# A layer of a graph network on Trainium2: three of six column chunks summed over fetched lists instead of by dense products

## The chip, the cores and the metric

The kernel runs on one core of a Trainium2 chip. A core has TensorE (PE, matmuls), VectorE (DVE), ScalarE (ACT), GpSimd (POOL) and SyncE (SP, which only issues DMAs here); each runs its instructions in order, and they meet through semaphores. The metric is the device time of one execution in microseconds. The kernel before took 2341.08 us, the median of three runs (2340.66 to 2345.28).

## The reference

There are N = 2708 nodes with D = 512 features. `adj` is a symmetric matrix of zeros and ones; about 0.6% of its entries are one. Four layers follow each other, each with a residual and a layer norm:

```python
x = _layernorm(x + _L0_gnn_ref(...))   # relu(((dinv (A+I) dinv) x + x) W + b)
x = _layernorm(x + _L1_gnn_ref(...))   # (dis A dis x) W.T + b
x = _layernorm(x + _L2_gnn_ref(...))   # two attention layers, softmax(scores) * adj
x = _layernorm(x + _L3_gnn_ref(...))   # A (x W) + b, heads side by side
```

Layer 3 can be computed as `(A x) W + b`: a sum of the neighbours' rows, then one product with a 512x512 matrix. That sum is what the change is about.

## The kernel before

The 2708 rows are cut into 22 blocks of 128 rows, the last with 20. The columns of A (the nodes that receive) are cut into six chunks of 512, 512, 512, 512, 384 and 276 (`CH`, L28). The blocks (the nodes that give) are taken in six groups of 4, 4, 4, 4, 3 and 3 (`GROUPS`, L30). A step is one chunk and one group, written (k, g) below.

*Dense sums.* Layers 0, 1 and 3 sum densely. `load` brings the bytes of A for a step, `prepare` turns them into weights `m` on ScalarE, and `multiply` (L849) accumulates, for each block and each of four slices of 128 features, two matmuls: one with the high and one with the low part of x (`xh`, `xl`). The result `acc` is the transposed sum. `evict` copies it to `ht`, `project` (L936) multiplies by W (`mm`), `combine` (L976) adds the residual `xres` and the bias, and `finish` does the layer norm and writes the rows. The bytes of A come from `masks`, written in layer 0.

*Lists.* The two attention layers do not sum densely. For each block of 128 receivers there are twelve lists of 128 givers: four with givers of the whole block and two for each quarter of 32 receivers; the last block has three lists. A list is fetched with one indirect DMA (`g<-pairs,givers`, a row per giver) on GpSimd, and multiplied with weights made from the row's softmax part. The indices of the givers (`givers`) are built during layer 1: `prepare` reduces the bytes of a group to one mark per giver and quarter (`feeds`, on VectorE), and after a chunk's last group `index` (L1097) ranks them, makes a one-hot table per block (`at_row`, `hit`, `both`, on VectorE) and multiplies it on TensorE (`list`). These jobs are spread over the following steps by `work`: one piece for VectorE or for TensorE after certain steps (`step`, L1043).

*Layer 1's surroundings.* In `step`, `before_products` first loads two steps ahead and prepares one step ahead, so VectorE's `feeds` reduce of step t+1 stands in its queue before what the step itself puts there: list tables, the ends of the chunk before (`combine`, LN), the evictions. On GpSimd's queue stand the writes of the finished rows (`x<-o`), of the transposed rows (`t<-x2t`, after ScalarE's copy) and the loads of the residuals (`xres<-x`). On TensorE's queue stand the dense products of the step, then a `list` product or transposes, then, at the chunk's end, the next chunk's.

*The tail.* While the second attention layer ends, `early` (L598) already runs the first twelve steps of layer 3: chunks 0 to 2 over groups 0 to 3; the half sums are copied away (`begun`). When the attention's last rows are there, `run` goes through the rest: groups 4 and 5 of chunks 0 to 2, then chunks 3 to 5 in full, all by `step`. Six chunk ends follow, each with four products with W per block and an LN of the chunk's blocks; the last chunk's three blocks are ended one by one after the last product.

*Order and memory.* Instructions are recorded through a wrapper (`Ordered`, L53), so that every instruction of this path has line L70 in the profile; they are told apart by the names of their tiles. Most tiles are pages of one ring of 82 (`PAGES`), fetched rows come into eleven wide tiles (`WIDES`), and the eight banks of the accumulator memory are split into two halves.

Of the kernel before, what the change touches and what calls it, by code (L numbers as in the profile page):

```python
# [41 lines left out]
PAGES, WIDES = 82, 11  # L42
TWO = 3
LN_EPS = 1e-5
DEG_EPS = 1e-8
SLOPE = 0.01


# [38 lines left out]
class Kernel:  # L87


    def __init__(self, ctx, tc, x_in, x_t, adj, adj_t, w0, b0, w1, b1, w2, w2_t, w3, b3, out):  # L90
# [26 lines left out]
        self.block = tile_("block", [P, NB], BF)  # L117
        self.since = tile_("since", [P, P], BF)
        self.saved = [
            [scratch.tile([P, D], FP, tag=f"x{s}_{i}", name=f"x{s}_{i}") for i in range(NB)]  # L120
            for s in range(3)
        ]
        self.between = [
            scratch.tile([P, D], FP, tag=f"y_{i}", name=f"y_{i}") for i in range(NB)
# [15 lines left out]
    def constants(self, page):  # L140
        nc = self.nc
        make_identity(nc, self.ident)
        nc.gpsimd.memset(self.ones, 1.0)
        nc.gpsimd.memset(self.ones_b, 1.0)
        nc.gpsimd.memset(self.feeds, 0.0)
        for q in range(QUARTERS):
            nc.gpsimd.memset(self.base[:, q : q + 1], float(q * ONLY * P - FAR))
        for dst, pattern, base, per_row in (
            (self.upto, [[1, P]], 0, 0),
            (self.node, [[0, 1]], 1 - P, 1),  # L150
            (self.block, [[1, NB]], 1 - NB, 0),
        ):
            w = dst.shape[1]
            whole = page("count", I32)[:, :w]
            nc.gpsimd.iota(whole, pattern=pattern, base=base, channel_multiplier=per_row)
            nc.gpsimd.tensor_copy(dst, whole)

        nc.gpsimd.memset(self.since, -1.0)
        nc.gpsimd.affine_select(
            out=self.since,  # L160
            in_=self.since,
            pattern=[[-1, P]],
            compare_op=ALU.is_ge,
            fill=0.0,
            base=0,
            channel_multiplier=1,
        )

    def load_w(self, pool, src, width, name, bufs=1):
# [344 lines left out]
class Fast:  # L514
# [17 lines left out]
    def run(self):  # L532
        kernel, nc = self.k, self.nc
        with ExitStack() as ctx:
# [23 lines left out]
            run.seq = [(l3, k, g) for k in range(TWO) for g in range(4)]  # L558
            run.seq += [(l3, k, g) for g in (4, 5) for k in range(2)]
            run.seq += [(l3, k, g) for k in range(2, TWO) for g in (4, 5)]  # L560
            run.seq += [(l3, k, g) for k in range(TWO, len(CH)) for g in range(len(GROUPS))]
            attention.run(self.early(run))
            for j in range(*GROUPS[5]):
                l3.rows[j] = attention.made[j]
            for t in range(4 * TWO, len(run.seq)):
                self.step(run, t)

            ly, k = run.before
            for i, n, ps in self.project(ly, k):
                self.finish(ly, k, [(i, n, self.combine(ly, i, n, ps))])  # L570

# [26 lines left out]
    def early(self, run):  # L598
# [7 lines left out]
        yield True  # L606
        for t in range(4 * TWO):
            ly, k, g = seq[t]
# [9 lines left out]
            self.prepare(*seq[t + 1])  # L618
            if g == 3:
                ly.begun[k] = []  # L620
            for n, j in enumerate(range(*GROUPS[g])):
                if t == 0:
                    self.multiply(ly, k, g, [j])
                else:
                    self.multiply(ly, k, g, ds=[n])
                self.attention.advance(2 * cost(CH[k][1]))
                if g == 3:
                    b = self.page(f"begun{k}_{n}")
                    self.nc.scalar.copy(b[:, : CH[k][1]], ly.acc[k][n][:, : CH[k][1]])
                    ly.begun[k].append(b)  # L630
                yield True


    def layernorm(self, rows):

# [9 lines left out]
        y = small.tile([P, DC], FP, tag="y", name="y")[:, :m]  # L645
        self.rsqrt(y, mv[:, :m, 1], LN_EPS)
        for q, (r, o, n) in enumerate(rows):
            nc.vector.tensor_scalar(
# [133 lines left out]
    def prepare(self, ly, k, g):  # L782
# [16 lines left out]
        if ly.number == 1:  # L799
            at, (j0, j1) = ly.done.pop(("bytes", k, g)), GROUPS[g]  # L800
            feeds = self.k.feeds.rearrange("p i q j -> p j (i q)")
            i0, full = c0 // QW, cw // QW
            sets = [(j0, j1, P)] if j1 < NB else [(j0, j1 - 1, P), (j1 - 1, j1, QW)]
            for q0, q1, n in ((0, full, QW), (full, -(-cw // QW), cw % QW)):
                for a, b, rows in sets if q0 < q1 else ():
# [5 lines left out]
                        ALU.max,  # L811
                    )

    def examine(self, ly, k, g, ats):
# [34 lines left out]
    def multiply(self, ly, k, g, only=None, ds=range(DC)):  # L849
        nc, cw = self.nc, CH[k][1]  # L850
        blocks = only or range(*GROUPS[g])
        two = ly.number == 3 and k < TWO
        starts, stops = ((0, 16), (15, NB - 2)) if two else ((0,), (NB - 2,))
        if blocks[0] in starts and 0 in ds:

            half = 0 if two and blocks[0] == 0 else k
            ly.acc[k] = [self.bank(half, f"acc{ly.number}_{k}_{d}") for d in range(DC)]
        ms = ly.done["m", k, g]
        if blocks[-1] == NB - 1:


            blocks = blocks[:-1]
            for x in (ly.hi, ly.lo):
                for d in range(DC):
# [4 lines left out]
                        ms[-1][few, :cw],  # L869
                        start=False,  # L870
                        stop=False,
                    )
        todo = [(d, j) for d in ds for j in blocks]
        if k == 0 and g + 1 < len(GROUPS):
# [61 lines left out]
    def project(self, ly, k):  # L936

        nc = self.nc
        parts = []
        for i, lo, n in blocks_of(k):  # L940
            if n <= QW:
                ps = self.few(
                    k,
                    f"mm{ly.number}_{i}",
                    n,
                    D,
                    lambda c: ly.ht[k][c][:, lo : lo + n],
                    lambda c: ly.w[c],
                )
                parts.append((i, n, ps))  # L950
                continue
            ps = self.bank(k, f"mm{ly.number}_{i}")
            for c in range(DC):
                nc.tensor.matmul(
                    ps[:n],
                    ly.ht[k][c][:, lo : lo + n],
                    ly.w[c],
                    start=(c == 0),
                    stop=(c == DC - 1),
                )  # L960
            parts.append((i, n, ps))
        return parts

    def residual(self, ly, k):
        for i, _, _ in blocks_of(k):
            t = self.page(f"xres{ly.number}_{i}")
            self.nc.gpsimd.dma_start(t, ly.source[i])
            ly.done["xres", i] = t

# [6 lines left out]
    def combine(self, ly, i, n, ps):  # L976

        nc, x = self.nc, ly.done.pop(("xres", i))
        if n <= QW:
            t = self.page(f"mm_sb{ly.number}_{i}")  # L980
# [13 lines left out]

    def finish(self, ly, k, parts):

        nc, out = self.nc, []
        for i, n, x in parts:
# [3 lines left out]
            out.append((i, o, n))  # L1002
        self.layernorm([(x, o, n) for (_, n, x), (_, o, _) in zip(parts, out)])
        for i, o, n in out:
# [270 lines left out]
class Attention:  # L1275
# [28 lines left out]
    def blank(self):  # L1304

        blank = [self.page(f"blank{e}") for e in range(2)]
        for e, t in enumerate(blank):
            self.nc.gpsimd.memset(t, 0.0)
            for pairs in (p for ly in self.pairs for p in ly):
                for r in range(2):  # L1310
                    c = e * D
                    w = min(D, D + 2 * P - c)
                    self.nc.sync.dma_start(pairs[r, N:, c : c + w], t[: NP - N, :w])

    def begin(self, step):
# [463 lines left out]


@with_exitstack
def kernel(
# [61 lines left out]
```

## Time and profile before

| what | us |
| --- | --- |
| median of three runs | 2341.08 |
| the profiled execution | 2338.2 |
| its span, first to last instruction | 2336.5 |
| TensorE busy | 2274.8 |
| VectorE busy | 1474.8 |
| GpSimd busy | 762.3 |
| ScalarE busy | 662.2 |
| mean granted TensorE clock | 0.993 |

The busy share of an engine is no measure of what bounds a stage; the chain of waits is: it follows the last instruction back, at each step to what released it. A row of the groups gives the line, the engine, the operation, the names of what is written and read with their shapes, the count, then busy time and mean, and after the second bar the idle time of the engine just before these instructions with its releaser. The largest group of GpSimd is the fetching of the attention layers:

```profile
L70 POOL DMA_INDIRECT g<-pairs,givers x510 | 516.2, 1012 | 897.0 <-DMA pairs<-s 537.4
```

Fetches come in a fixed rhythm where nothing holds them, here at the end of the second attention layer in GpSimd's timeline (start, length, what, and in brackets the idle time before):

```profile
2095.87 0.95 POOL L70 DMA_INDIRECT g<-pairs,givers  x1 [0.30 <-PE acc L70]
2097.12 0.94 POOL L70 DMA_INDIRECT g<-pairs,givers  x1 [0.30 <-PE acc L70]
2098.37 0.95 POOL L70 DMA_INDIRECT g<-pairs,givers  x1 [0.30 <-issue]
```

### The profile page before, as it was taken

How to read it: one execution, taken by the hardware profiler on the slowest of the kernel's cores; microseconds unless marked ns; L12 is line 12 of the kernel's file. 1: busy time of each engine (PE TensorE's matmuls, PEld its weight loads, DVE VectorE, ACT ScalarE, POOL GpSimd, SP SyncE). 2: the span in 40 equal slices, each digit the busy share in tenths (PEclk: the TensorE clock that was granted, in tenths of full speed). 3: DMA queues.
4: the chain of work that ended last, by engine and by line, in shares of the span. 5: the costliest groups of instructions: out<-in, count | busy, mean ns of one | idle time of the engine just before them, and what ended most of it. 6: DMA issues, size and time to landing. Idle time of an engine off the chain costs nothing.

```text
span 2336.5 us, 26171 instructions
## 1 busy us (share of the span) xinstructions
PE 2274.8 (97%) x8518; PEld 1292.5 (55%) x8518; DVE 1474.8 (63%) x2831; ACT 662.2 (28%) x1334; POOL 762.3 (33%) x879
## 2 busy tenths in 40 slices
PE   8999999999999999999999999999999999999997
PEld 6677677778644444443456444444443456566585
DVE  6999986786655529657677511228677788724523
ACT  6544353223100113222223200113232334432211
POOL 6645641111000000636375550000636466551000
PEclk9999999999999999999999999999999999999998
DMA  9765652222434404869699996405869799983311
GB/s 343 258 199 169 182 172 86 74 86 70 171 146 167 154 0 143 278 229 311 204 324 350 302 388 232 152 0 163 279 217 314 233 316 329 305 279 96 123 48 43
DMA packets 312440, 463.50 MB, mean 198 GB/s; under 512 B 60162, under 2 KB 189706, under 8 KB 312292
## 3 DMA queue, kind: packets, MB, share of 16 engines
q1 hardware_dynamic: 252276, 240.81, 31.5%
q0 software_dynamic: 60016, 220.92, 27.1%
q8 instruction: 69, 1.13, 0.2%
q14 instruction: 79, 0.65, 0.1%
HBM read 307.75 MB, written 153.85 MB: 198 GB/s over the span
## 4 chain that ended last, share of the span: by engine, by line
PE 84%; DVE 7%; DMA 4%; issue 2%; ACT 1%; POOL 1%; SPq 0%; DVEq 0%; ACTq 0%; POOLq 0%
PE sp L70 32%; PE acc L70 29%; PE mm L70 9%; PE z L70 6%; PE wst L70 6%; DMA pairs<-s 1%; DMA at<-in_adj_t 1%; DVE st L70 1%; DMA at<-mask 1%; ACT m L70 1%; DVE s L70 1%; PE list L70 1%; PE mix L70 0%; POOL bytes L70 0%; PE tr_x2t L70 0%
## 5 line engine op out<-in xcount | busy, mean ns | idle before, releaser
L70 POOL DMA_INDIRECT g<-pairs,givers x510 | 516.2, 1012 | 897.0 <-DMA pairs<-s 537.4
L70 PE MATMUL sp<-xs,wst_sb 128*128 128x512 f32 (+3 forms) x2112 | 797.7, 544 | 0.0
L70 PEld LDWEIGHTS sp<-xs,wst_sb 128*128 128x128 f32 (+1 forms) x2112 | 380.0, 186 | 406.8 <-issue 321.9
L70 PE MATMUL acc<-m,xh 128*128 128x512 f32 (+4 forms) x1584 | 571.4, 382 | 13.6 <-ACT m L70 7.0
L70 PE MATMUL acc<-m,xl 128*128 128x512 f32 (+4 forms) x1584 | 553.2, 367 | 1.5 <-DVE xl L70 1.5
L70 PEld LDWEIGHTS acc<-m,xh 128*128 128x128 f32 (+1 forms) x1584 | 290.3, 189 | 81.4 <-issue 22.3
L70 PEld LDWEIGHTS acc<-m,xl 128*128 128x128 f32 (+1 forms) x1584 | 290.3, 189 | 48.1 <-issue 5.7
L70 ACT COPY s<-sp 128x512 f32<-128x512 f32 (+2 forms) x252 | 133.6, 531 | 482.1 <-PE sp L70 469.5
L70 PE MATMUL acc<-g 128*32 128x512 f32 (+1 forms) x1020 | 260.8, 605 | 0.9 <-DMA g<-pairs,givers 0.5
L70 DVE TENSOR_TENSOR top<-top,s 128x512 f32<-128x512 f32 (+5 forms) x240 | 149.6, 623 | 170.6 <-ACT s L70 169.1
L70 PE MATMUL mm<-w,ht 128*128 128x512 f32 (+1 forms) x528 | 222.6, 593 | 8.1 <-DVE ht L70 8.1
L70 ACT CAST m<-at 128x512 fp32r<-128x512 uint8 (+5 forms) x396 | 199.2, 567 | 80.0 <-DMA at<-mask 63.7
L70 ACT ACTIVATE s<-s 128x512 f32<-128x512 f32 (+3 forms) x264 | 150.7, 580 | 236.6 <-DVE s L70 236.3
L70 DVE TENSOR_TENSOR sum<-sum,s 128x512 f32<-128x512 f32 (+4 forms) x252 | 157.4, 625 | 23.9 <-ACT s L70 23.9
L70 DVE TENSOR_TENSOR s<-s,a 128x512 f32<-128x512 f32 (+3 forms) x264 | 165.9, 628 | 10.2 <-DMA a<-mask 1.2
L70 DVE TENSOR_TENSOR s<-s,shift 128x512 f32<-128x512 f32 (+3 forms) x264 | 162.8, 620 | 6.7 <-ACT shift L70 6.7
L70 PEld LDWEIGHTS mm<-w,ht 128*128 128x128 f32 (+1 forms) x528 | 95.5, 186 | 124.4 <-issue 110.9
L70 PE MATMUL wst<-xt,mixed 128*128 128x512 f32 (+2 forms) x384 | 152.5, 550 | 1.7 <-ACT mixed L70 1.7
L70 PEld LDWEIGHTS acc<-g 128*32 128x32 f32 (+1 forms) x1020 | 75.4, 134 | 136.9 <-issue 115.8
L70 PE MATMUL z<-w,xt 128*128 128x512 f32 (+1 forms) x352 | 151.0, 596 | 0.0
L70 DVE COPY z_sb<-z 128x512 f32<-128x512 f32 (+1 forms) x44 | 30.3, 690 | 179.5 <-PE z L70 176.3
L70 POOL DMA_DIRECT2D x<-o x44 | 26.0, 596 | 358.0 <-DVE o L70 354.2
(167 smaller groups left out, 1657.4 us busy)
## 6 DMA issues: line engine op xcount, KB each, us to landing
pairs<-s SPq DMA_DIRECT2D x378, 128.0 KB
pairs<-z_sb SPq DMA_DIRECT2D x84, 512.0 KB
at<-in_adj_t SPq DMA_DIRECT2D x84, 256.0 KB
xres<-x POOLq DMA_DIRECT2D x44, 256.0 KB, 4.3
x<-o POOLq DMA_DIRECT2D x43, 256.0 KB, 3.1
x<-x SPq DMA_DIRECT2D x37, 256.0 KB
at<-mask SPq DMA_DIRECT2D x32, 256.0 KB
xt<-t SPq DMA_DIRECT2D x32, 256.0 KB
```

The source lines that it names most:

```text
L70: ins = call(*args, **kw)
```

## The change

Chunks 3, 4 and 5 of layer 3 are no longer summed densely. Their sums go over the lists that the attention layers already use.

*Rows with masks.* The input of layer 3 is kept in one table `rows3` of 586 columns: 512 of x, then 32 + 24 + 18 words. A word holds sixteen bits of A's row, for sixteen receivers of chunks 3 to 5, as an integer. So one fetched row brings a giver's features and whom it gives to.

*Making the words.* In layer 1, `prepare` calls `words` for chunks 3 to 5 in place of the `feeds` reduce: GpSimd multiplies the weights `m` with powers of two, VectorE adds each sixteen of them up and copies the sums to integers, then makes `feeds` as the maximum of two sums, and GpSimd writes the integers to `rows3`. The powers are made once in layer 0 (`bits`).

*The tail.* `early` takes one more step, (2, 4). The class `Listed` then runs the lists of the last ten blocks; the generator `rest` holds what is left of chunks 0 to 2, and `Listed.run` interleaves the two by a clock of estimated times. For a list: an indirect fetch of 128 rows; VectorE's `bitwise_and` of the word of each row with the sixteen bits (`hit`); ScalarE's copy to floating point (`both`); a matmul with the fetched rows. As a set bit counts 2^r for receiver r of a word, the sum is scaled by 2^-r (`unbit`) when ScalarE copies it out. It is then transposed, copied and multiplied with W. Blocks end in pairs, with the last pass of the layer norm on ScalarE. Layer 3's residual loads move from GpSimd's queue to SP's, and its dense sums now use one half of the banks, the lists the other.

```diff
+LISTED = (3, 4, 5)
+WORD = 16
+ROW = D + sum(-(-CH[k][1] // WORD) for k in LISTED)
...
+        self.rows3 = scratch.tile([NP, ROW], FP, tag="rows3", name="rows3")
+        self.saved.append([self.rows3[i * P : (i + 1) * P, :D] for i in range(NB)])
...
+    def bits(self, page):
...
+        for r in range(WORD):
+            nc.gpsimd.memset(powers[:, r : r + 1], float(2**r))
+        nc.gpsimd.tensor_copy(self.bits_b, powers[:, :WORD])
+        nc.gpsimd.tensor_copy(self.bits_i, powers[:, :WORD])
...
-            run.seq += [(l3, k, g) for g in (4, 5) for k in range(2)]
-            run.seq += [(l3, k, g) for k in range(2, TWO) for g in (4, 5)]
-            run.seq += [(l3, k, g) for k in range(TWO, len(CH)) for g in range(len(GROUPS))]
+            run.seq.append((l3, TWO - 1, 4))
+            run.early = len(run.seq)
+            run.seq += [(l3, k, g) for k in range(TWO) for g in (4, 5) if g == 5 or k < TWO - 1]
             attention.run(self.early(run))
...
-            for t in range(4 * TWO, len(run.seq)):
-                self.step(run, t)
...
+            listed = Listed(self, l3)
+            listed.run(self.rest(run, listed))
...
+    def rest(self, run, listed):
+        for t in range(run.early, len(run.seq)):
+            ly, k, g = run.seq[t]
+            self.before_products(run, t)
+            for d in range(DC):
+                self.multiply(ly, k, g, ds=[d])
+                listed.advance(3 * 2 * 0.226)
+                if d % 2:
+                    yield True
+            if g == 4:
+                continue
+            self.residual(ly, k)
+            self.biased(ly, k)
+            self.evict(ly, k)
+            yield True
+            for i, n, ps in self.project_blocks(ly, k):
+                listed.advance(DC * cost(D))
+                listed.later(2.0, lambda a=(i, n, ps): listed.end(*a))
+                yield True
...
+            if k in LISTED:
+                self.words(k, ms, sets, feeds)
+                return
...
+    def words(self, k, ms, sets, feeds):
...
+        for a, b, rows in sets:
+            for e in range(a, b, 2):
...
+                        nc.gpsimd.tensor_tensor(
+                            to, at.bitcast(FP), powers.to_broadcast([rows, q1 - q0, n]), ALU.mult
+                        )
+                    nc.vector.tensor_reduce(
+                        sums[:rows, e - j0 : e - j0 + m, q0:q1],
+                        prod[:rows, :m, span].rearrange("p j (w r) -> p j w r", r=n),
+                        AX.X,
+                        ALU.add,
+                    )
+            f, w = (t[:rows, a - j0 : b - j0, :nw] for t in (sums, whole))
+            nc.vector.tensor_copy(w, f)
...
+            nc.vector.tensor_reduce(
+                feeds[:rows, a:b, i0 : i0 + nw // 2],
+                f.rearrange("p j (q w) -> p j q w", w=2),
...
+            nc.gpsimd.dma_start(to.rearrange("(j p) w -> p j w", p=rows), w.bitcast(FP))
...
+class Listed:
...
+    def weigh(self, wait=False):
...
+        hit, both = tile_("hit", I32), tile_("both", FP)
+        for h, g in enumerate(gs):
+            o = word_at(i, h if side else 0)
+            nc.vector.tensor_tensor(
+                hit[:, h * m : (h + 1) * m, :],
+                g[:, o : o + m].bitcast(I32).unsqueeze(2).to_broadcast(shape),
+                self.k.bits_i.unsqueeze(1).to_broadcast(shape),
+                ALU.bitwise_and,
+            )
+        nc.scalar.copy(both, hit)
+        weights = both.rearrange("p w r -> p (w r)")
+        for h, g in enumerate(gs):
+            lo, rows = (h * QW, QW) if side else (0, n)
+            nc.tensor.matmul(
+                self.acc[lo : lo + rows],
+                weights[:, lo : lo + rows],
+                g[:, :D],
...
+        self.advance(1.1 if side else cost(D))
+        if last:
+            self.later(1.5, lambda a=(i, n, self.acc): self.turn(*a))
...
+    def run(self, products):
+        while True:
+            if self.weigh() or next(products, False):
+                continue
+            if self.pending:
+                self.advance(self.pending[0][0] - self.clock)
+            elif not self.weigh(True):
+                return
```

## The prediction

> **What bounds the kernel now.** I read the page's busy table first, then the chain of waits by engine, then the chain of the last 200 us in order of time, then the groups of instructions by shape, and last the timelines and stretches of the two places that the change touches: layer 1 (about 480 to 660 us) and the tail (2140 us to the end).
>
> ```profile
> PE 2274.8 (97%) x8518; PEld 1292.5 (55%) x8518; DVE 1474.8 (63%) x2831; ACT 662.2 (28%) x1334; POOL 762.3 (33%) x879
> ...
> PE 84%; DVE 7%; DMA 4%; issue 2%; ACT 1%; POOL 1%; SPq 0%; DVEq 0%; ACTq 0%; POOLq 0%
> ```
>
> TensorE is busy 97% of the span and carries 84% of the chain. So matmuls removed come off the time, unless TensorE then waits; and wherever TensorE is made to wait in layer 1, the wait is paid in full.
>
> ```profile
> 2178.78 11.78 PE acc L70 x54
> 2190.56 13.73 PE mm L70 x32
> 2204.29 37.31 PE acc L70 x176
> 2241.60 13.73 PE mm L70 x32
> 2255.34 28.38 PE acc L70 x176
> 2283.72 10.30 PE mm L70 x24
> 2294.02 18.10 PE acc L70 x144
> 2312.12 3.45 PE mm L70 x8
> ```
>
> This is the tail, from the chain: start, length, what, how many. `acc` are the dense sums of layer 3, `mm` the products with W. TensorE does one after the other with no gap. The dense sums of chunks 3, 4 and 5 are 32 of the first 54 (32 x 0.228 = 7.3 us), then 37.3, 28.4 and 18.1: 91 us. A product with W costs 13.73/16 = 0.86 us per 128x512 matmul.
>
> ```profile
> 480.00:540.00 60.00, 60.00 (x333) 44.77 (x332) 48.61 (x92) 15.98 (x37) 6.62 (x12) 1.00 0.24 74
> 540.00:600.00 60.00, 60.00 (x304) 45.60 (x303) 41.16 (x86) 11.20 (x29) 6.09 (x11) 1.00 0.36 110
> 600.00:660.00 60.00, 60.00 (x312) 35.26 (x309) 34.12 (x72) 8.49 (x25) 5.57 (x10) 1.00 0.42 154
> ```
>
> Layer 1 in stretches of 60 us; the columns are PE, PEld, DVE, ACT, POOL busy, then clock and DMA. TensorE is full; VectorE has 48.6 of 60 in the first stretch, so it is the engine with little slack; GpSimd has only 6 us of work. But GpSimd's few instructions sit in a line that the change lengthens:
>
> ```profile
> 509.51 1.27 POOL L70 DMA_DIRECT2D x<-o  x2 [45.64 <-DVE o L70]
> 512.47 1.08 POOL L70 DMA_DIRECT2D x<-o  x2 [1.68 <-issue]
> 516.05 2.13 POOL L70 DMA_DIRECT2D t<-x2t  x4 [2.50 <-ACT x2t L70]
> 518.17 2.14 POOL L70 DMA_DIRECT2D xres<-x  x4
> ```
>
> And the prices, from the groups by shape (count, then busy and mean ns):
>
> ```profile
> L70 POOL TENSOR_TENSOR xt<-xt,dg 128x512 f32<-128x512 f32 x16 | 20.2, 1289 | 21.8 <-DVE cnt_sb L70 21.8
> L70 POOL TENSOR_TENSOR xt<-xt,dg 128x384 f32<-128x384 f32 x4 | 3.9, 1002 | 2.0 <-DVE cnt_sb L70 2.0
> L70 POOL TENSOR_TENSOR xt<-xt,dg 128x276 f32<-128x276 f32 x4 | 3.0, 790 | 0.0
> ...
> L70 DVE TENSOR_REDUCE feeds<-at 128x64 bf16<-128x2048 uint8 x16 | 36.5, 2284 | 0.0
> ...
> L70 DVE TENSOR_REDUCE feeds<-at 128x32 bf16<-128x1024 uint8 x8 | 9.7, 1218 | 0.0
> ```
>
> **What the Trainium skill says.** "GPSIMD Engine Reference", section "Performance versus the Vector engine", puts elementwise two-input work on VectorE and GpSimd well behind it. The trace agrees: 1289 ns on GpSimd for 128x512 against 0.69 on VectorE. "DMA: Bandwidth & Descriptors", section "Anatomy of one DMA — SWDGE (gpsimd) path", says that a DMA issued from GpSimd has its descriptors built there in software. The trace agrees for the indirect fetches, which keep GpSimd for 0.95 us each; but its table of queues counts only 60016 software packets, about the rows of 510 fetches, so GpSimd's plain DMAs go by hardware, and still take 0.55 us of its time each. I rest no other step on a page.
>
> **The change, part by part.**
>
> *Bits and masks of constants.* 32 memsets on GpSimd of about 0.12 us (the 128x1 memsets of the trace), two copies, two small VectorE operations and one DMA, early in layer 0. 4 us of GpSimd beside a TensorE that is full there. 0; at worst +4 if the mask writes behind them come late.
>
> *Layer 1, chunks 3 to 5: words().* The VectorE reduce of a group (2.28 us) goes. In its place, per group of four blocks: four GpSimd products (4 x 1.29 = 5.2 us), two VectorE reduces of 1024 elements (2 x 1.22), a copy to integers and a small maximum (about 0.5), and a DMA on GpSimd with 512 short pieces (about 0.8, as the mask DMAs). VectorE's own cost is 2.9 against 2.3, nothing much. What counts is the order. VectorE's reduce waits for GpSimd's products; GpSimd's DMA waits for VectorE's integers, and the next group's products stand behind that DMA. One round is 5.2 + 1.2 + 0.5 + 0.8 = 7.7 us, one after the other, against 4 x 8 x 0.228 = 7.3 us that TensorE needs for the group. Over a chunk that is 4 x 7.7 + 2 x 6.4 = 44 us, plus the 6.6 us of DMAs shown above and their idle time (2 to 4 us), in a period of about 62 us: GpSimd as a whole fits, but not where the groups follow fast. Behind VectorE's waiting reduce stand the one-hot tables of the list building (4.1 us each), the LN of the chunk before, and the evictions of the finished sums; TensorE waits for each of these in program order (`list` matmuls after groups 3, 4 and 5 of a chunk; `wst` and products after the evictions). And behind GpSimd's waiting DMA stand `x<-o`, `t<-x2t` and `xres`.
>
> My walk through the queues with these durations, TensorE's order unchanged: lists after (3,3) +1 us, after (3,4) +3 in all, after (3,5) +8.5; in chunk 4 most of it is only kept, since the products of 384 columns are shorter (1.00 us), but its evictions stand behind words of (5,0): +6.5, 15 in all; in chunk 5 the transposes wait for `o` (+3, 18 in all) and the last list for its table (+6): 24. I take +24 us. Bounds: if the bf16 output brings the product near 0.7 us, a round is 5.4 us, shorter than the group, and some +5 stay; if GpSimd and VectorE also slow each other, +45. I take the f32 row, since one input is f32, and the shape is the nearest.
>
> *Tail: TensorE.* Removed: 91 us. Added: nine blocks of twelve lists, four of them whole (4 x 0.86) and two sets of four quarters (a set of four ran in about 1.3 us in the attention), 6.04 each, 54.4; three lists of the last block, 2.6: 57 us. 40 transposes at 0.12 us (16 took 1.91) and switches: 6 us. Products with W stay. Net 57 + 6 - 91 = -28 us.
>
> *Tail: the end.* Before, VectorE ran combine and LN of three blocks after the last matmul, 2315.6 to 2329.0 = 13.4 us. After, the order ends with a pair: two adds 1.4, statistics 1.8, root 1.5, the scaling on ScalarE 1 to 1.5: about 6.5, -7. In front of the last product with W, TensorE now waits for copy, transposes, copy (0.6 + 0.5 + 0.6 and the hops): +4. Net -3.
>
> *Tail: fetching.* 111 indirect fetches, 1.25 us apart as in the attention before, 139 us. The last rows of attention are written at about 2127, so the last fetch is issued near 2266 and lands 6 us later, while TensorE has 150 us of work from 2138 on (57 lists, 41 + 32 products, 6, 14 dense). It fits, with 15 us to spare: 0; if a fetch of 2344 bytes per row goes at 1.5 us apart, +12. The residual loads go to SP's queue, which has little to do: 0.
>
> *Tail: waits within.* Each list needs one VectorE instruction (the bit test) and one ScalarE copy before its matmuls, with two buffers. VectorE is in order, and LN of a pair (2 x 0.7 + 3.3 us), the four biases and four evictions of a chunk (5.5 us) stand before the next bit test. Two buffers cover about 2 x 1 us of matmuls. The dense sums and products that the planner puts between lists cover part. By hand: 4.7 us at the first pair, 1.5, 3.5 and 4 at the evictions, the rest in pieces of below 1: +18 (from 0, all covered, to +28).
>
> Tail: -28 - 3 + 18 = -13 us. Both: +24 - 13 = +11. On the span that is 2336.5 + 11 = 2347.5, on the profiled execution's time (1.7 above its span) 2349; the median of before is 2.9 above its profiled execution, so 2352 on that basis.
>
> **The rivals.**
>
> *B: the words are hidden (faster).* One mechanism: the ping-pong of GpSimd and VectorE stays inside TensorE's period, since there are 60 us for 50 of GpSimd; the product comes out at about 0.7 to 0.9 us and the first waits never add up. For it: GpSimd has 6 of 60 us now. Against: VectorE is at 48.6 of 60, in order, and waits. Then layer 1 costs +3 and the tail brings -25 (its waits half covered): 2341 - 22 = 2319. It decides as soon as a round is below the 7.3 us of TensorE's group, that is a product below about 1.1 us.
>
> *C: the tail gives nothing, layer 1 costs what I say (slower).* Bit tests behind LN on VectorE at each block, or fetches at 1.5 us, give TensorE gaps as large as the 28 us that it saves. For it: one fetch per list and one bit test per list, both in order; chains of five engines per block. Against: 15 us of slack in fetching. 2341 + 24 + 1 = 2366.
>
> *D: the two cancel (no change).* Half of the wait in layer 1 (+12) against -13: 2340.
>
> **How the numbers follow.** A change of less than 0.2%, 4.7 us, is what this measurement can't tell from none. Forecast (A, 2352, own range 2344 to 2372) 0.44; B 0.36; C 0.13; D 0.07. Slower is A and C, 0.57; faster is B and a little of D, 0.36; same 0.07. The range 2310 to 2376 reaches to B's lower part (tail -28, layer 1 near 0) and to C; it leaves out layer 1 at +45 and a tail at -35.
>
> **What would show it.** In the profile after: products on GpSimd at 1.29/1.0/0.8 us and TensorE's `list` rows with idle time released by VectorE in layer 1; the start of the attention's scores later than before by 24 us (B: within 3). In the tail: no `acc` of chunks 3 to 5, fetches 1.25 us apart, list matmuls waiting for `both`; the stretch from the attention's last row to the end shorter by 13 us (B: 25 or more; C: none). I am wrong if a round of GpSimd and VectorE is clearly shorter than TensorE's group, or if VectorE gets the words done in its slack ahead of the tables.

## The result, and the profile after

The changed kernel takes 2394.18 us (2391.07 to 2398.9) where the kernel before takes 2340.87: 1.0227 of it, with a 95% interval of 1.0204 to 1.025. That is 53 us more. The forecast had the sign and the larger place of the loss, but its 2352 us is short by 42, and the time lies outside its own range of 2344 to 2372.

The page's table of busy times, in the form of the one shown of the kernel before:

```profile
PE 2270.4 (95%) x8252; PEld 1240.2 (52%) x8252; DVE 1520.6 (64%) x3006; ACT 674.9 (28%) x1364; POOL 942.4 (39%) x1111
```

266 matmuls are gone, and yet TensorE is busy for only 4.4 us less. The change moved work off TensorE, and TensorE runs what is left more slowly and with gaps.

Three landmarks in the traces show where the 57.4 us between the two spans (2336.5 and 2393.9) lie: the start of the first and of the last run of `list` products, which bound layer 1, and the end of the last product over a fetched list in the attention.

| stretch | before | after | difference |
| --- | --- | --- | --- |
| start to the first list product | 414.4 | 417.6 | +3.2 |
| layer 1: first to last list product | 398.0 | 438.5 | +40.5 |
| to the last product of the attention | 1304.1 | 1306.5 | +2.4 |
| tail: from there to the end | 220.1 | 231.4 | +11.3 |

Layer 1 in the same stretches of 60 us (columns PE, PEld, DVE, ACT, POOL busy, then TensorE's clock and the DMA share):

```profile
480.00:540.00 60.00, 53.02 (x241) 37.92 (x241) 53.70 (x88) 12.83 (x27) 24.56 (x27) 0.93 0.21 62
540.00:600.00 60.00, 54.47 (x282) 43.62 (x282) 46.91 (x80) 13.35 (x33) 34.90 (x41) 0.93 0.25 72
600.00:660.00 60.00, 45.60 (x297) 36.09 (x296) 42.36 (x106) 11.32 (x33) 36.66 (x69) 0.87 0.55 156
```

TensorE was full here before, with a clock of 1.00. Now it stands still for 27 of 180 us, and its clock is 0.87 to 0.93. The groups by shape name who lets it wait, first of TensorE (before and after), then of GpSimd:

```profile
L70 PE MATMUL list<-both,at_row 128*128 128x24 bf16 x484 | 15.6, 173 | 4.2 <-DVE both L70 4.2
...
L80 PE MATMUL list<-both,at_row 128*128 128x24 bf16 x484 | 15.7, 174 | 21.9 <-DVE both L80 21.9
```

```profile
L80 POOL TENSOR_TENSOR prod<-m,bits_b 128x512 bf16<-128x512 f32 x21 | 24.0, 1177 | 6.4 <-ACT m L80 6.3
L80 POOL DMA_DIRECT2D rows<-wi x21 | 16.0, 760 | 66.0 <-DVE feeds L80 39.1 <-DVE wi L80 15.5 <-DVE place_r L80 11.4
```

The `list` products wait 21.9 us for VectorE's one-hot tables (4.2 before). GpSimd waits 66 us for VectorE in front of its writes of the words. This is the order that the prediction had named. What it had not seen is in VectorE's timeline, with GpSimd's of the same time below it (start, length, what):

```profile
570.10 0.74 DVE L80 SCALAR_TENSOR_TENSOR r<-mm,dis,bias 128x512 f32<-128x512 f32 x1
570.88 4.33 DVE L80 TENSOR_TENSOR xres<-xres,r 128x512 f32<-128x512 f32 x1
575.13 0.74 DVE L80 SCALAR_TENSOR_TENSOR r<-mm,dis,bias 128x512 f32<-128x512 f32 x1
575.90 0.69 DVE L80 TENSOR_TENSOR xres<-xres,r 128x512 f32<-128x512 f32 x1
```

```profile
571.14 3.51 POOL L80 TENSOR_TENSOR prod<-m,bits_b 128x384 bf16<-128x384 f32 x4
```

The same addition takes 4.33 us and then 0.69. The long one begins 0.26 us before GpSimd's four products and ends 0.56 us after the last of them: it stands still for as long as GpSimd multiplies. I call this the standstill. The longest wait of TensorE in layer 1, 6.86 us in front of the `list` product at 538.06, comes in the same way. These are the three one-hot tables that VectorE makes for it, and GpSimd's products of that time:

```profile
529.66 7.33 DVE L80 TENSOR_TENSOR at_row<-upto,row 128x1024 bf16<-128x1024 bf16 x3
```

```profile
532.80 3.37 POOL L80 TENSOR_TENSOR prod<-m,bits_b 128x512 bf16<-128x512 f32 x3
```

In the kernel before, three such tables take 3.4 us (1216, 1216 and 950 ns). Not every instruction of VectorE is held. Some of those that lie beside a product of GpSimd in this layer:

| instruction | beside a product, ns | alone, ns |
| --- | --- | --- |
| `xres<-xres,r`, two operands | 814 to 5296 (4 of them) | 692 |
| `whole<-place`, one operand, to integers | 744 and 4871 | 200 (before) |
| `both<-hit,node`, one operand | 752 (one) | 292 |
| `wf<-prod`, a sum, of 128x768 and of 128x544 | 948 (3) and 717 (7) | 947 and 714 |
| `r<-mm`, one operand in the accumulator memory | 751 (one) | 746 |

So the number of operands does not decide it: of these, the sums and what reads the accumulator memory go on, and the others stand still, those with one operand too.

The Trainium skill, "Advanced Engine Details and Errata", section "VectorE Performance Modes", says that VectorE's second port to its memory is shared with GpSimd, and that GpSimd's instructions and VectorE's in its two-port modes block each other. This trace agrees, and shows it for a plain f32 addition of two operands too (4.33 us for 0.69). That the port is the reason is the page's word: the trace shows the standing still alone.

The tail's waits of TensorE (who waits, for what, us in total, times, the longest):

```profile
PE acc L80 <- ACT both L80: 16.9, 14, 4.3
PE mm L80 <- DVE ht L80: 13.7, 1, 13.7
PE tr L80 <- ACT sum L80: 4.2, 2, 3.4
PE acc L80 <- ACT xh L80: 4.1, 1, 4.1
```

Fourteen waits for the lists' weights make up 16.9 us, and one single wait 13.7. The chain, in order of time, shows what that one is:

```profile
2306.64 0.54 SPq L80
...
2307.28 11.55 DMA xres<-rows
2318.85 0.04 DVE xres L80
...
2319.46 0.70 DVE ht L80
2320.20 5.38 PE mm L80 x8
```

Residual rows are issued late on SP, load for 11.55 us beside the fetches, and VectorE's bias and evictions and TensorE's products stand behind them. The eight products that follow take 5.38 us; eight such products took 3.45 in the kernel before.

### The profile page after: what moved, and what is told of

Same layout as the page of the kernel before. It is cut to its first block, busy times and chain, and to the rows that moved or that the text cites. A ratio compares the mean times of both kernels' runs of the same rounds, so it can differ in the third digit from the quotient of the medians.

```text
span 2393.9 us, 26363 instructions
## 1 busy us (share of the span) xinstructions
PE 2270.4 (95%) x8252; PEld 1240.2 (52%) x8252; DVE 1520.6 (64%) x3006; ACT 674.9 (28%) x1364; POOL 942.4 (39%) x1111
## 4 chain that ended last, share of the span: by engine, by line
PE 62%; DVE 4%; DMA 4%; ACT 1%; issue 1%; SPq 0%; POOL 0%; ACTq 0%; DVEq 0%; POOLq 0%
PE sp L80 31%; PE acc L80 14%; PE z L80 6%; PE wst L80 6%; PE mm L80 3%; DMA pairs<-s 1%; DMA g<-pairs,givers 1%; DVE st L80 1%; DMA at<-mask 0%; DMA xres<-rows 0%; DVE r L80 0%; PE tr_x2b L80 0%; DMA a<-mask 0%; PE den L80 0%; DVE xres L80 0%
## 5 line engine op out<-in xcount | busy, mean ns | idle before, releaser
L80 PE MATMUL acc<-m,xh 128*128 128x512 f32 (+3 forms) x1320 | 492.3, 393 | 21.4 <-DVE place_r L80 7.7
L80 PE MATMUL acc<-m,xl 128*128 128x512 f32 (+3 forms) x1320 | 475.8, 377 | 5.3 <-DVE xl L80 5.3
L80 PEld LDWEIGHTS acc<-m,xh 128*128 128x128 f32 (+1 forms) x1320 | 246.1, 192 | 87.8 <-issue 22.1
L80 PEld LDWEIGHTS acc<-m,xl 128*128 128x128 f32 (+1 forms) x1320 | 246.1, 193 | 49.1 <-DVE xl L80 8.2
L80 PE MATMUL mm<-w,ht 128*128 128x512 f32 (+1 forms) x448 | 199.2, 611 | 19.1 <-DVE ht L80 19.1
L80 ACT CAST m<-at 128x512 fp32r<-128x512 uint8 (+5 forms) x330 | 171.4, 576 | 76.4 <-DMA at<-mask 32.9
L80 PEld LDWEIGHTS mm<-w,ht 128*128 128x128 f32 (+1 forms) x448 | 83.9, 193 | 127.2 <-issue 98.7
L80 POOL DMA_INDIRECT g<-rows,givers x111 | 107.0, 964 | 105.3 <-PE acc L80 36.1
```

Source lines behind the costliest of these rows:

```text
L80: ins = call(*args, **kw)
```

## The experiments

Two theories for layer 1. The *mutual wait*: VectorE's sum waits for GpSimd's product, GpSimd's write waits for VectorE, and the rest waits behind them in order. The *standstill*: VectorE's instructions (sums and readers of the accumulator memory apart) stand still beside GpSimd's products, whoever waits. A third, VectorE's amount of work, is tested with them. For the tail: order of the queues, or too little other work beside the lists.

The runs below were on two other chips, on which the kernel before takes 2363 to 2367 and 2370 to 2371 us; the attention alone is 20 to 34 us longer there than in the first trace of the kernel before. So they are compared by their ratio to the kernel before on their own chip and by the stretches of the table above, each from one trace. Layer 1 repeats well: four traces with the words unaltered give 438.5 to 439.3 us. The tail does not: seven traces with it unaltered give 231 to 239 us, so a difference of less than 8 us between two traces of it says nothing. Unaltered, the changed kernel was on the second chip:

> The changed kernel unaltered, so that the others of this set have it beside them on the same chip: 1.02 to 1.025 of the kernel before.

It gave 1.0262 (1.0225 to 1.0299), layer 1 438.5 us as on the first chip, and a tail of 236.6 us.

**Without words.** `words` is not called, the marks come from the old reduce, and the words in the table stay zero.

```diff
-            if k in LISTED:
-                self.words(k, ms, sets, feeds)
-                return
...
```

> Leaves out the making of the mask words in layer 1 (the marks come from the old reduce, the words in the table are zeros, so the sums of chunks 3 to 5 are empty); the tail is as in the changed kernel. If the loss is what TensorE loses in layer 1 (about 40 us between the list products there) plus 11 us in the tail: 2394 - 40 = 2354 us, with TensorE full from 470 to 690 us again. If layer 1 is not the cause of that (the lateness comes from layer 0 or the DMAs): above 2380.

1.0083 (1.0054 to 1.0112). Layer 1 takes 397.3 us, as before. So all of the 40 us belong to the words. Of the 20 us that remain, 11 are the tail (231 us; 220 in the first trace of the kernel before).

**Products on VectorE.**

```diff
-                        nc.gpsimd.tensor_tensor(
+                        nc.vector.tensor_tensor(
```

> The products of mask and powers run on VectorE instead of GpSimd, nothing else. VectorE gets some 36 us more work, GpSimd 66 us less. Theory of the mutual wait (VectorE's sum waits for GpSimd's product, GpSimd's write for VectorE) and theory of the standstill (VectorE's two-operand instructions stand still while GpSimd's products run) both say that most of the 40 us comes back: layer 1 costs 5 to 15, so 2359 to 2369 us, and the one-hot, residual and place instructions on VectorE take their old durations. If VectorE's amount of work is the bound in layer 1: 2394 or above.

1.0154 (1.0118 to 1.0189); layer 1 412.7 us, 25.8 less than in the changed kernel. VectorE's amount of work is not what costs the 40 us: with some 36 us of products more on it, TensorE loses less. The instructions that stood still are back at their old durations, as VectorE's groups in layer 1 show:

```profile
L80 DVE TENSOR_TENSOR xres<-xres,r 128x512 f32<-128x512 f32 x13 | 9.0, 693 | 0.4
...
L80 DVE TENSOR_TENSOR at_row<-upto,row 128x768 bf16<-128x768 bf16 x8 | 7.6, 948 | 0.0
```

These are the same rows, in the same window of 465 to 690 us, in the kernel before and in the changed one:

```profile
L70 DVE TENSOR_TENSOR at_row<-upto,row 128x768 bf16<-128x768 bf16 x10 | 9.5, 950 | 0.0
L70 DVE TENSOR_TENSOR xres<-xres,r 128x512 f32<-128x512 f32 x13 | 9.0, 692 | 0.4
...
L80 DVE TENSOR_TENSOR xres<-xres,r 128x512 f32<-128x512 f32 x11 | 16.4, 1488 | 0.4
L80 DVE TENSOR_TENSOR at_row<-upto,row 128x768 bf16<-128x768 bf16 x8 | 13.1, 1636 | 0.0
```

For the 14.7 us that stay, VectorE's longer queue is the likely reason: TensorE's four longest new gaps (1.5, 3.4, 1.9 and 2.1 us) all end on VectorE.

**Sums one step later.** The products stay on GpSimd; VectorE's sums and GpSimd's write of a group are issued after the next group's products.

```diff
-                self.words(k, ms, sets, feeds)
+                todo = self.words(k, ms, sets, feeds)
+                self.flush()
+                self.unfinished.append(todo)
...
```

> VectorE's sums of a group and GpSimd's write stand one step later, behind the products of the next group; GpSimd still makes the products. Theory of the mutual wait: nobody waits any more, 25 to 35 us come back, 2360 to 2370 us. Theory of the standstill: GpSimd's products lie beside the same amount of VectorE work as before, so at most 10 us come back, 2384 to 2394 us; residual additions still at about 1.5 us instead of 0.69.

1.0209 (1.0178 to 1.024); the interval overlaps that of the changed kernel, but layer 1 is clear with 421.4 us, 17.1 less. Neither number was hit: more came back than the standstill alone allows, and less than the mutual wait alone promises. In VectorE's groups the waits are mostly gone (9.5 us in the last row in the changed kernel, 1.3 here), and the standstill is not:

```profile
L80 DVE TENSOR_TENSOR xres<-xres,r 128x512 f32<-128x512 f32 x13 | 17.7, 1362 | 0.4
L80 DVE TENSOR_TENSOR at_row<-upto,row 128x768 bf16<-128x768 bf16 x8 | 12.4, 1549 | 0.0
...
L80 DVE TENSOR_REDUCE wf<-prod 128x48 f32<-128x768 bf16 x10 | 9.2, 946 | 1.3 <-POOL prod L80 1.3
```

**Products that nobody reads.** The sums, the write and the early `return` are taken out, and the words in the table stay zero; GpSimd's products stay.

```diff
             if k in LISTED:
                 self.words(k, ms, sets, feeds)
-                return
...
-                    nc.vector.tensor_reduce(
-                        sums[:rows, e - j0 : e - j0 + m, q0:q1],
...
-            nc.vector.tensor_copy(w, f)
...
-            nc.gpsimd.dma_start(to.rearrange("(j p) w -> p j w", p=rows), w.bitcast(FP))
...
```

> GpSimd makes the products of masks and powers in layer 1 as in the changed kernel, but nobody reads them: no sums on VectorE, no write of words, the marks come from the old reduce, the words in the table are zeros. So no instruction waits for a product. Theory of the standstill: VectorE's two-operand instructions beside the products still take two to four times their time, TensorE loses 15 to 25 us between the first and the last list product of layer 1 (423 to 413 us for that stretch, against 398 before and 439 in the changed kernel). Theory of the mutual wait: nothing is lost, 398 us.

1.0146 (1.0108 to 1.0183); layer 1 411.2 us, 13 more than before and 14 more than without words, from which it differs by the products alone. Nothing reads a product. GpSimd's own writes and loads still stand behind them in its queue, but between 430 and 850 us no wait of VectorE, ScalarE or TensorE ends on GpSimd, and TensorE's three new gaps (2.3, 1.1 and 5.7 us) end on VectorE's `up` and `both`. That leaves the standstill. The 13 us are a little less than the range given. GpSimd suffers as well: its product of 128x512 takes 1498 ns here on the mean, 1177 in the changed kernel. The groups of VectorE and of GpSimd in layer 1:

```profile
L80 DVE TENSOR_TENSOR at_row<-upto,row 128x768 bf16<-128x768 bf16 x9 | 12.7, 1410 | 0.0
```

```profile
L80 POOL TENSOR_TENSOR prod<-m,bits_b 128x512 bf16<-128x512 f32 x21 | 30.9, 1498 | 14.7 <-DVE up L80 6.8 <-ACT m L80 6.3 <-DVE whole L80 1.3
```

**Words without GpSimd.** Four bytes are packed at a time by shifts and ors on VectorE.

```diff
...
+            one(t, v, 7, v, ALU.logical_shift_right, ALU.bitwise_or)
+            one(t, t, 14, t, ALU.logical_shift_right, ALU.bitwise_or)
+            nc.vector.tensor_single_scalar(t, t, 15, op=ALU.bitwise_and)
...
+            one(w, q[:, :, :, 1], 4, q[:, :, :, 0], ALU.logical_shift_left, ALU.bitwise_or)
+            for e in (2, 3):
+                one(w, q[:, :, :, e], 4 * e, w, ALU.logical_shift_left, ALU.bitwise_or)
...
```

> The words are made on VectorE from the bytes themselves, four bytes at a time, with shifts and ors on 32-bit integers: six small instructions for a group, no product on GpSimd, no sum over sixteen. VectorE's work for a group is about 3.4 us, 1.1 us more than in the kernel before. If GpSimd's products (standing still and waiting) are the whole loss in layer 1, the stretch from the first to the last list product is 400 to 406 us (before 398, changed 439, products on VectorE 413), about 35 us less than the changed kernel: 1.010 to 1.013. If anything else in the words costs (the writes of the integers on GpSimd's queue, the small reduce), it stays above 415.

1.0087 (1.0058 to 1.0116); layer 1 398.1 us against 398.0 before. VectorE is busier there than before (288 us of 442, 267 before), so that much more work costs nothing, nor do the writes of the words on GpSimd's queue: the loss was GpSimd's products and what waits for them.

**Residual rows one chunk earlier.**

```diff
+        self.residual(run.seq[-1][0], 0)
...
-            self.residual(ly, k)
             self.biased(ly, k)
             self.evict(ly, k)
+            if k + 1 < TWO:
+                self.residual(ly, k + 1)
```

> Only the tail: the residual rows of chunks 0 to 2 of layer 3 are loaded one chunk earlier, so that on SP's queue they no longer stand behind a write of rows that ScalarE has yet to make. If the 13.7 us gap of TensorE in front of chunk 2's products with W comes from that order, it goes, with the slow clock behind it: 2394 - 15 = 2379 us. If the load is slow because the fetches fill the DMA engines, VectorE still waits for it or for the next one: 2390 or above.

1.0238 (1.0211 to 1.0266), beside 1.0262 of the changed kernel on that chip, which was measured in another set; these intervals overlap, so the trace has to decide. The long gap is no more (the largest one left in that place is 3.2 us): it came from the order on SP's queue. The tail is 227.8 us instead of 236.6, and TensorE's gaps in it are 10 us shorter. So about 9 of the 15 us came, not all; where the rest went, two traces of a tail that varies by 8 us don't tell.

**And five buffers for the weights.** This comes on top of the edit before.

```diff
-            [P, len(ts) * m, WORD], dt, tag=tag, name=f"{tag}3_{i}", bufs=2
+            [P, len(ts) * m, WORD], dt, tag=tag, name=f"{tag}3_{i}", bufs=bufs
...
+        hit, both = tile_("hit", I32, 2), tile_("both3", FP, 5)
```

> Tail only: residual rows one chunk earlier, and five buffers instead of two for the weights that ScalarE makes for the lists (one page fewer in the ring). If in-order waits behind two buffers are what TensorE's gaps in the tail are made of, the tail becomes 18 to 25 us shorter than in the changed kernel. If the fetches set the pace (1.25 us each), no more than 10 us, which the residual rows bring alone.

1.0226 (1.0184 to 1.0267); this interval too overlaps that of the changed kernel. The tail is 221.0 us, 15.6 less than in the changed kernel on that chip; but the same tail takes 229.7 us in the run with both repairs below, on the third chip, and by the median times the gain is 9 us. So the 18 to 25 us of the buffers did not come, and no more than the residual rows' 9 is shown. The gaps of 0.9 to 1.1 us before many lists stay, and so does the one of 4.3 us after the first pair: VectorE and ScalarE work in order (in the changed kernel the bit tests for it begin after the layer norm, at 2207.50, and the copy after ScalarE's scaling, at 2209.05), and no number of buffers lets a bit test pass what stands before it.

**Words made during the attention.** `tail2`, and products and sums on VectorE from bytes that are fetched again, a group at a time, between the projections of the second attention layer.

```diff
             for _ in self.project_steps(ly, k):
+                if not any(c.to_weigh for c in self.chunks):
+                    next(words, False)
                 yield True
+        for _ in words:
+            pass
...
```

> As tail2, and the words are not made in layer 1: the bytes of A are fetched again while the second attention layer makes its projections, where VectorE has 15 to 20 of 100 us of work and GpSimd none, and VectorE makes products and sums there. Layer 1 is then as before (398 us), the words cost nothing if VectorE's slack there holds them (some 85 us in 200) and 5 to 15 us if the evictions behind them keep TensorE waiting. Sum: 35 us less than tail2, about the time of the kernel before (0.995 to 1.005).

A miss: 1.0424 (1.039 to 1.0458). Layer 1 is at 398.1 us as expected, but the attention is 1424.8 us instead of about 1330. The lists of the first attention layer are only done late (its last fetch is at 1423 us, the first product of words at 1440), and 70 of the 136 products of words came in one heap in the last 60 us; TensorE waits once for 57.0 us and once for 13.1 for VectorE. The slack was there as a mean over 200 us, not at the point where the words stood in the queue.

**Both repairs together.** Integer words and `tail2`; then with chunk 3 dense again, after the leftovers or before them.

> int_words and tail2 together. The two parts don't share anything, so their gains add: about 45 us less than the changed kernel, 1.004 to 1.010 of the kernel before; the tail still has gaps of some 30 us.

1.0049 (1.0033 to 1.0066), as expected: the gains add.

```diff
-LISTED = (3, 4, 5)
+LISTED = (4, 5)
...
+            run.seq += [(l3, TWO, g) for g in range(len(GROUPS))]
```

> As best2, but only chunks 4 and 5 go over lists; chunk 3 is summed densely in the tail and stands beside the lists as work that TensorE can do while a list isn't ready. TensorE has about 14 us more to do than in best2 (40 for the dense sums, less 24 for lists and 2 for transposes). If the gaps of the tail come from too little other work beside the lists, 10 to 20 of their 30 us go and the time is 5 us around that of best2. If they come from chains within a block that nothing covers, it is 10 us slower than best2.

1.0002 (0.9982 to 1.0022), better than either theory had said: TensorE's gaps in the tail are 22.6 us instead of 38.1, although chunk 3 stands at the end. That fewer lists simply mean fewer chains is likely, but was not tried apart.

```diff
-            run.seq += [(l3, k, g) for k in range(TWO) for g in (4, 5) if g == 5 or k < TWO - 1]
             run.seq += [(l3, TWO, g) for g in range(len(GROUPS))]
+            run.seq += [(l3, k, g) for k in range(TWO) for g in (4, 5) if g == 5 or k < TWO - 1]
```

> As best3, but the dense sums of chunk 3 come first in the tail and the leftovers of chunks 0 to 2 after them; so they cover the 6 us in which TensorE waits for the last rows of the attention to come back, and the lists have this work beside them. If the gaps of best3's tail (22 us) come from too little other work at its beginning, 6 to 12 us go with the slow clock behind them: 0.995 to 0.998 of the kernel before. If they come from the order within VectorE's queue, the same gaps appear further on: 1.000.

0.9972 (0.9961 to 0.9982): 0.3% faster than the kernel before (2363.89 against 2370.66 us on that chip, from 22 and 26 executions), and the only one of these kernels that is faster at all. The tail is 208.7 us instead of 218.6. With the order, the residual loads and the splitting of the last rows of x moved too. The start of the tail shows it:

```profile
2151.77:2200.00 48.23, 47.53 (x203) 32.02 (x203) 15.02 (x45) 16.34 (x38) 23.84 (x25) 1.00 0.68 216
2200.00:2250.00 50.00, 42.00 (x150) 21.16 (x148) 15.01 (x53) 14.80 (x38) 28.69 (x30) 0.97 0.72 220
```

In the first 48 us after the attention TensorE is busy for 47.5 at full clock; in the changed kernel it was busy for 36.8 of the first 47.5 us at a clock of 0.87.

## Why the prediction was wrong

*The direction and the order of the parts* were right: layer 1 loses more than the tail could bring. The forecast A was the nearest of its cases, and rival B, words hidden in GpSimd's slack, is refuted: the round of GpSimd and VectorE did not fit under TensorE's group.

Three terms of the sum were wrong. The spans differ by 57.4 us where 11 were forecast, 46 too little. The slower clock behind TensorE's gaps was not in the sum at all, and is 11 us in layer 1 and 9 in the tail. The move of the residual loads was put at 0 and made one wait of 13.7 us. The waits in layer 1 are 29 us where 24 were forecast. The start and the attention, 5.6 us longer, were put at 0 too; for these the cause stays open.

*Layer 1, +24 forecast, +40.5 measured.* The step that failed is the walk through the queues "with these durations". It took VectorE's durations of the kernel before for VectorE beside GpSimd's products. They don't hold there: the same addition has a mean of 1488 ns instead of 692, the last one-hot table of a block 1636 instead of 950. I had this only as the bound "if GpSimd and VectorE also slow each other, +45" and gave it no place in the range; 40.5 is close to it. The walk named the right places: TensorE's new gaps are 12.4 us at the lists of chunk 3 (8.5 forecast), 9.1 where chunk 5 begins (6.5) and 5.3 at the last list (6); the transposes' 3 us did not come, and 2.3 us came near the beginning of chunk 3. That the gaps' sum of 29 us lies near 24 is in part luck, since the standstill was not in the walk, and alone made 9 us of gaps where nobody read a product. The price of a GpSimd product was right for chunks 3 and 4 (1177 and 1047 ns against 1289 and 1002); in chunk 5 a block takes two, of 272 and 4 columns, 743 and 243 ns against 790. Rival B's condition, a product below about 1.1 us, was worked out for the 512 columns of chunk 3 and was not met there. The parts can be bounded, not added up: the standstill alone costs 13 us, taking the waits away brings 17, taking GpSimd out brings 26, and shortening the work on VectorE too brings all 40.

*The clock: a term that was missing.* Of the 40.5 us, 29 are gaps of TensorE (2.3, 6.9, 0.7, 4.9, 1.4, 7.7 and 5.3 us); the other 11 are matmuls that ran longer. After the gap of 6.86 us at 531 to 538, and after the one of 4.85 us before 556.66, stretch by stretch (same columns as above):

```profile
538.00:541.50 3.50, 3.44 (x29) 2.86 (x30) 3.46 (x7) 1.74 (x4) 1.23 (x2) 0.50 0.00 0
541.50:546.00 4.50, 4.40 (x19) 3.25 (x17) 4.46 (x4) 0.00 (x0) 4.04 (x6) 0.96 0.80 198
...
557.00:560.50 3.50, 3.50 (x26) 3.50 (x23) 2.65 (x6) 3.05 (x8) 1.98 (x3) 0.50 0.23 56
```

Behind five of the seven gaps the granted clock is one half, for 3.4 to 5.7 us; behind those of 0.7 and 1.4 us it is not. In layer 1 TensorE is busy for 29.3 us at half clock, 6.8 before. Half of the difference is 11.2 us, which is what the gaps leave of the 40.5. The Trainium skill states such a rule, in "TensorE: Matmul & The Clock Gate", section "Part 1: The HAM clock gate (the "warmup" mystery)": an idle window of about 3.4 us halves the clock, and so long a busy one restores it. The trace agrees in the length of the slow time, but shows it after shorter gaps as well. After one of 2.26 us, 25 matmuls took 6.2 us instead of 4.6, and in the kernel before the clock is 0.50 from 416 to 419 us, behind a gap of 1.24 us. The length of the gap alone does not decide: behind a gap of 2.68 us in front of the last `list` products the clock stays at 1.00 in both kernels, and with the unread products it falls to 0.50 behind the same gap. I had not priced a stall of TensorE so.

*The tail, -13 forecast, +11.3 measured.* Two terms failed. The first is the move of the residual loads to SP's queue, costed at 0 because SP "has little to do". What counted was not the amount but what stands ahead: a write of finished rows that waits for ScalarE, and behind it loads that VectorE needs before the evictions. That made the wait of 13.7 us, and moving the loads forward removed it. The second is the clock again. The saving of TensorE, -28, came as -20 of busy time. The step that `early` takes more moved nothing out of this stretch: 377 dense matmuls of layer 3 stand before the landmark in both traces. But 20.8 us of TensorE's busy time in the tail are at half clock, 3.4 before, so 8.7 us were lost that way, about the difference.

The waits within, +18 forecast, were about right for what they meant: the waits for `both` are 16.9 us. In all, the idle time of TensorE up to its last matmul rises from 5.3 us to 41.4: 16.9 for `both`, 13.7 for the residual rows, 4.9 for `sum` and `turned` (+4 forecast) and 5.9 for the attention's last rows (`xh`, `xl`).

The end was about as forecast in size, not in its working: from the last matmul to the end of the span 11.5 us instead of 16.5, -5 for -7. The 13.4 us that the forecast called VectorE's work after the last matmul begin at 2315.6 us, where the products of the first of the last three blocks end; TensorE went on with the other two until 2319.96.

*The fetches* were costed rightly: 111 of them, 1.25 us apart where nothing holds them. TensorE's waits in the tail are for `both`, not for fetched rows, and VectorE's bit tests wait for fetched rows for 5.6 us in all.

*GpSimd's plain DMAs* were misread, though no term of the sum rests on it. The prediction says that they go by hardware, since the table of queues counts 60016 software packets. But between 505 and 525 us of the kernel before GpSimd issues twelve plain DMAs of 256 KB and no fetch, and the table for that stretch (queue, packets, MB, share) has their 3.1 MB as software packets:

```profile
q0 software_dynamic: 951, 3.13, 46.8%
```

So the trace agrees with the cited page of the Trainium skill for plain DMAs too; the page has this in its section "SWDGE vs HWDGE vs iDMA".

*The bits*, forecast at 0 with +4 as the worst, stand in a layer 0 that is 3.2 us longer; the other kernels with integer words have it too (2 to 3 us), but no run was without them, so that part is not shown.

## What to carry to other kernels

Before work is given to an idle GpSimd, look at what VectorE does at that time: additions, comparisons and conversions in its own memory stood still beside GpSimd's products here, so GpSimd's slack is not free, and a shorter formula on VectorE can be cheaper than one on GpSimd. Price a stall of a full TensorE at its length plus what half clock behind it costs: over the seven gaps of layer 1, 29 us of gaps drew 11 us of it. Let a dense piece of work stand beside a chain of short dependent ones. When a DMA is moved to another queue, ask which instruction ahead of it there has to wait, not how busy the queue is.

## What was not expected of the hardware

- A VectorE addition of 128x512 that meets four GpSimd products lasted 4.33 us instead of 0.69: it waited out all four, not one. A conversion that met eight short products (`whole<-place`, 744 ns for 200) got in between them.
- Conversions with one operand stood still too (up to 4871 ns); sums and what reads the accumulator memory did not (948 for 947 ns, 751 for 746).
- The standstill goes both ways: GpSimd's product took 1177 ns with VectorE often waiting for it, and 1498 on the mean, up to 3785, where it ran free beside VectorE.
- A gap of TensorE of 1.24 us can be enough for the half clock behind it, and one of 2.68 us need not bring it.
